# Norm statistics of an MLP's first pass: from the scheduler's places to fixed turns behind the change of pairs

## The chip, the core and the metric

The kernel runs on one core of a Trainium2 chip. The metric is the device time of one execution in microseconds (us). The engines are called by the names of the profile: PE is the matrix engine (TensorE), DVE is VectorE, ACT is ScalarE, POOL is GpSimd, and SP is the engine that issues most of the transfers (DMAs). Each engine works through its own instructions in order and waits where an instruction needs a result of another engine.

## The reference

The input x has 4 sequences of 1024 rows with 128 columns. Four blocks follow each other, each adding its result to x:

```
x = x + attention(layernorm(x))     # 16 heads of 8; each row sees the last 32 rows
                                    # and every 64th row before it; softmax
x = x + mlp(layernorm(x))           # "pass a": 128 (as x and -x) -> 512 -> 512 -> 128, weights +1 or -1
x = x + mamba(x)                    # a state-space block: norm, projection, convolution, a scan
                                    # over time with 16 states, gate, projection, its own residual
x = x + mlp(layernorm(x))           # "pass b" and "pass c": the same MLP again
```

A layernorm needs two numbers of each row, its mean and its variance; the row is then scaled by (variance + 1e-5) to the power -1/2 and shifted. These two numbers are the statistics that this case is about: those of the MLP's first pass, over x as the attention has left it.

## The kernel before

**Tiles.** x stays on the chip. The sequences form two pairs; a tile is 128 partitions, which hold 64 rows of each of the pair's two sequences, by 128 columns, and each pair has 16 such tiles, `xs[0]` and `xs[1]`. Four neighbouring tiles form a chunk (c = 0 to 3 in a pair).

**Attention.** The function `attention` (L201) runs a pipeline written out by hand, the loop at L546 over turns i. In turn i it works on several tiles at once, at different stages: the scores and the softmax of tile i, the strided products of tile i-1, the weights of tile i-2, the values of i-3, the division of i-4 and the residual of i-5, which adds the projected result to x. The tiles 0 to 15 are those of the first pair and 16 to 31 those of the second, so pairs change at turn 16, and tile t of the first pair is final behind the residual in turn t+5. In a pair's tile m the products with every 64th row have m columns of heads: POOL's multiplications (`product`, rows prod; `strided_products`, rows prodv) and DVE's sums over them (rows S<-prod and or<-prodv) grow with m from nothing to 15 x 128 elements, and start again at nothing when the pair changes. prod and prodv share three buffers, so POOL cannot run far ahead of DVE. On DVE a turn is: the predicated copy of the scores S (L395), the reciprocal and product of `divide`, the sums of `strided`, the product eo of `weights_own`, the residual, and `softmax_scores` (L406): the sum S<-prod, the maximum mx, the subtraction S<-S,mx. ACT then makes the exponentials E. Behind that stand the statistics of the attention's own norm for a later chunk (`stats`, L244: a `bn_stats` and a `bn_aggr` for one tile a turn, rows sta and mva; `scales`, L254: four POOL operations for a chunk, rows rsa).

While `attention` is traced, the helper `InOrder` (L49, flag `keep`) asks the scheduler to keep the program's order. The code behind it is traced without that until the scans.

**The MLP.** `mlp` (L685) is a generator that yields a Piece before each group of instructions. Pass a over the first pair is four units, `early(0, c, ...)` for c = 0 to 3 (L784), two in each of two lanes (L1289). Without given statistics it first runs `ln_stats` (L181), which yields four pieces: `bn_stats` and `bn_aggr` on DVE for the chunk's four tiles (two pieces, rows st_fa and mv_fa, L177 and L178), four POOL operations (one piece, rows rs_fa, L187 to L190) and an empty piece. Then come the scaled tiles (fxna), their transposes (ftpa), the first layer (pfa, evicted to h1a), the second (pga, to h2a), the third (pfoa) and the residual (x<-pfoa). The units of the second pair, `early(1, c, ...)`, have their statistics made ahead by `stats_ahead` (L776) and wait for them in `awaited` (L780), a single piece.

As the four units of the first pair stand in no kept order, the scheduler moves their statistics up to where their input is final: tile t's `bn_stats` and `bn_aggr` lie in turn t+5 on DVE, between the operations of `softmax_scores`, and each chunk's four POOL operations lie behind the chunk's last tile, at 72, 105, 139 and 160 us.

**The prologue.** Behind the attention, at L1301, the two lanes and the first units of the mamba block (`mamba_norm`, `mamba_pre_half`, rows mtp, mxn, pc, px, pd, dt, du) are run in turn, a piece of each at a time, until the first mamba unit is prepared. This interleaving counts pieces. It is not by time, and it ends when the scans can start.

**The scans.** `scans` (L1083) goes through 128 units (8 parts of half a sequence x 16 states). For each, POOL makes db, ACT da, DVE two scans hs and a product hc (with pcc from PE), POOL sums pairs of hc, and PE adds these up (pys). Between the units, `pieces` (L1244) places what is left of the MLPs and the other mamba units, by a planner with costs for each engine, in a fixed order. What is still left when the last unit has been placed comes behind it: the tail, with the last mamba output (pmo), and the last MLP units. The transposes of these units are the rows ftpc.

The names that the change and the steps of the prediction touch: `ln_stats`, `early`, `awaited`, `known` (L774), the loop at L546, and the interleaving at L1307. The lines that say how many pieces go in turn:

```python
            wanted = first[-1].may() and "pe" in first[-1].next.us
            for w in first + ([] if wanted else lanes):
                if w.may():
                    w.run()
```

Of the kernel before, what the change touches and what calls it, by code (L numbers as in the profile page):

```python
# [16 lines left out]
F32 = mybir.dt.float32  # L17
# [5 lines left out]
ALU = mybir.AluOpType  # L23
# [3 lines left out]
P = 128  # L27
# [3 lines left out]
NT = T // R  # L31
# [4 lines left out]
EPS = 1e-5  # L36
# [7 lines left out]
def hybrid_kernel(ctx: ExitStack, tc: tile.TileContext, x, Wq, Wk, Wv, Wo, ln_g, ln_b, W_in, conv_w,  # L44
# [17 lines left out]
    ve, te, sc, gp = (InOrder(e) for e in (nc.vector, nc.tensor, nc.scalar, nc.gpsimd))  # L62
    const = ctx.enter_context(tc.tile_pool(name="const", bufs=1))
    xpool = ctx.enter_context(tc.tile_pool(name="xpool", bufs=1))
    small = ctx.enter_context(tc.tile_pool(name="small", bufs=4))
# [15 lines left out]
    xs = []  # L81
    for bp in range(NP):
        t = xpool.tile([P, NT, C], F32, tag=f"x{bp}", name=f"x{bp}")
# [22 lines left out]
    def load_mlp():  # L106
        for t, k in ((k0s, k0), (k1s, k1), (k2s, k2)):
            nc.sync.dma_start(t, k.rearrange("(i p) f -> p i f", p=P))
        for i, s in enumerate((s0, s1, s2, res_scale)):
            nc.sync.dma_start(scal[:, i : i + 1], s.partition_broadcast(P))  # L110
# [35 lines left out]
    minus_half = const.tile([P, 8], F32, name="minus_half")  # L146
# [47 lines left out]
    def ln_apply(dst, src, scale, bias):  # L194
        for i in range(src.shape[1]):
            sc.activation(
                dst[:, i, :], src[:, i, :], AF.Identity, bias=bias[:, i : i + 1], scale=scale[:, i : i + 1]
            )


    def attention(actx):  # L201
# [32 lines left out]
        def weights_in():  # L234
            wt = spare("wt")
            for i in range(4):
                te.transpose(wt[:, i * C : (i + 1) * C], wsrc[:, i], ident)
            sc.copy(wqkv.rearrange("p i c -> p (i c)"), wt[:, : 3 * C])
            sc.copy(woT, wt[:, 3 * C :])
# [4 lines left out]
        def stats(cc, tiles_of=range(4)):  # L244
            bp, c = divmod(cc, NT // 4)
            if cc not in sums:
                sums[cc] = small.tile([P, 4, 2], F32, tag="mva", name=f"mva{cc}", bufs=2)
            mv = sums[cc]
            for i in tiles_of:
                st = small.tile([P, 6], F32, tag="sta", name=f"sta{cc}_{i}", bufs=2)  # L250
                ve.bn_stats(st, xs[bp][:, 4 * c + i, :])
                ve.bn_aggr(mv[:, i, :], st)

        def scales(cc):  # L254
            mv = sums.pop(cc)
            rs = norms[cc] = small.tile([P, 2, 4], F32, tag="rsa", name=f"rsa{cc}", bufs=2)
            gp.tensor_scalar_add(rs[:, 0], mv[:, :, 1], EPS)
            gp.tensor_tensor(rs[:, 0], rs[:, 0], minus_half[:, :4], ALU.pow)
            gp.tensor_scalar_mul(rs[:, 1], mv[:, :, 0], -1.0)
            gp.tensor_mul(rs[:, 1], rs[:, 1], rs[:, 0])  # L260
# [92 lines left out]
        def scores(i):  # L353

            bp, m = tiles[i]
            qT, kx = prep[i // 4][:2]
            q0 = i % 4 * P
            before_tile = prep[(i - 1) // 4][1][:, (i - 1) % 4] if m else None
            ps = psum["s", i] = pw.tile([P, H, 2, W], F32, name=f"ps{i}", tag="ps")
            for g in range(4):  # L360
                rows = slice(g * W, (g + 1) * W)
                for hf in range(2):
                    ch = slice(hf * 64, hf * 64 + 64)
                    heads = slice(hf * HB, (hf + 1) * HB)
                    q = qT[ch, q0 + g * W : q0 + (g + 1) * W]
                    te.matmul(
                        ps[rows, heads, 0, :], q, kx[ch, i % 4, :, g * W : (g + 1) * W], start=True, stop=True
                    )
                    if g % 2:
                        before = kx[ch, i % 4, :, (g - 1) * W : g * W]  # L370
                    elif m:
                        before = before_tile[ch, :, (g + 1) * W : (g + 2) * W]
                    else:
                        continue
                    te.matmul(ps[rows, heads, 1, :], q, before, start=True, stop=True)
            S[i] = ap2.tile([P, H, W + NT - 1], F32, name=f"S{i}", tag="S")

        def keep_scores(i):
            sc.copy(S[i][:, :, :W], psum["s", i][:, :, 0, :])
# [97 lines left out]
        def spread_values(cc, heads):  # L477
            vr = prep[cc][3]
            for a in heads:
                rows = slice(a * W, (a + 1) * W)  # L480
                src = vr[rows].rearrange("k g (j a d) -> k (g j) a d", j=4, d=HD)
                dst = vbs[cc % 2][rows].rearrange("k g j c -> k (g j) c")[:, :, :W]
                dst = dst.rearrange("k j (a d) -> k j a d", d=HD)
                sc.copy(dst[:, :, a], src[:, :, a])
# [53 lines left out]
            ve.tensor_add(xs[bp][:, m, :], xs[bp][:, m, :], psum.pop(("y", i))[:, :C])  # L538


        LEAD = 7

        starts = {(3 if cc == 1 else 4 * cc) - LEAD: cc for cc in range(len(tiles) // 4)}
        preps = []
        last = len(tiles)
        for i in range(-LEAD, last + 5):  # L546
            def at(k, stage):
                if 0 <= i + k < last:
                    stage(i + k)

            if i == -LEAD:
                weights_in()
            if i == 0:
                load_mlp()
            at(-1, strided_products)
            at(1, product)
            at(-2, weights)
            at(0, scores_before)
            at(-4, divide)
            at(-2, strided)  # L560
            at(-2, weights_own)
            at(-2, weights_all)
            at(-2, weights_before)
            at(-5, project_out)
            at(-5, residual)
            if i == 3 - LEAD:
                scores(0)
                keep_scores(0)
            if i >= 0:
                at(1, scores)  # L570
                at(1, keep_scores)
            at(0, softmax_scores)
            at(0, softmax_exp)
            if i in starts:
                preps.append(prep_steps(starts[i]))
            for p in preps:
                next(p, None)
            at(-4, turn_out)
            at(-3, values)
            at(-4, keep_out)  # L580
            for p in preps:
                next(p, None)
            cc, step = divmod(i + LEAD, 4)
            if cc + 2 < last // 4:
                stats(cc + 2, range(step, step + 1))
                if step == 3:
                    scales(cc + 2)
            cc, step = divmod(i + 1, 4)
            if 0 <= cc < last // 4:
                spread_values(cc, range(step, step + 1))  # L590

    with ExitStack() as actx:
        keep.append(True)
        attention(actx)
        keep.clear()
# [89 lines left out]
    def mlp(u, tiles, split, pool, lane, own=None, soon=False, hasty=False, stats=None):  # L685
# [32 lines left out]
        yield Piece(sc=1.6)  # L718
        xn = fx.tile([P, nt, C], F32, name=f"fxn{u}", tag=f"fxn{lane}", bufs=1)
        ln_apply(xn, tiles, stats[:, 0], stats[:, 1])  # L720
        yield fill(0.8)
        tp = bank(f"ftp{u}")[:, :cols]
# [47 lines left out]
        xc = tiles.rearrange("p m c -> p (m c)")  # L770
        ve.scalar_tensor_tensor(xc, po, total, xc, ALU.mult, ALU.add)


    known = {}  # L774

    def stats_ahead(key, needs, tiles_of, soon=False):  # L776
        yield Piece(ready=lambda: all(k in fed for k in needs), same=True)
        known[key] = yield from ln_stats(tiles_of(), "f" + "_".join(map(str, key)), soon)

    def awaited(key):  # L780
        yield Piece(ready=lambda: key in known, same=True)
        return known[key]

    def early(bp, c, *args):  # L784
        stats = (yield from awaited(("a", bp, c))) if bp else None
        tiles = xs[bp][:, 4 * c : 4 * c + 4, :]
        yield from mlp(f"a{bp}_{c}", tiles, True, *args, hasty=bp == 1 and c < HALF, stats=stats)
        fed.add(("a", bp, c))
# [78 lines left out]
    def mamba_norm(bp, c):  # L867
# [21 lines left out]
        yield Piece(sc=1.6)  # L889
        xn = fx.tile([P, 4, C], F32, name=f"mxn{u}", tag="mxn", bufs=1)  # L890
        ln_apply(xn, tiles, rs[:, 1], rs[:, 3])
        if c % HALF == 0:

# [7 lines left out]
        for i in range(4):  # L901
            te.transpose(tp[:, i * P : (i + 1) * P], xn[:, i, :], ident)
        yield Piece(sc=1.6, same=True)
        ln_apply(tiles, tiles, rs[:, 0], rs[:, 2])
        yield evict(sc=0.6)
        t0 = DC - 1 + c % HALF * 4 * R
# [376 lines left out]
    def in_scan_buffers(u):  # L1283
# [5 lines left out]
    lanes = [  # L1289
        Work(stream(  # L1290
            early(0, lane, f1, lane, *[in_scan_buffers] * lane),
            early(0, 2 + lane, f1, lane),
            early(1, lane, f1, lane),
            early(1, 2 + lane, f1, lane),
            *(late(0, 2 * q + lane, f1, lane) for q in range(CT // 2)),
# [95 lines left out]
```

## Time and profile before

| What | us |
| --- | --- |
| median of 4 executions | 908.99 |
| lowest and highest | 908.34 and 911.04 |
| the profiled execution's own time | 911.04 |
| its span, from the first to the last instruction | 909.3 |
| last residual of the attention begins | 247.4 |
| first scan (hs) begins | 323.86 |
| last product of the scans (hc) begins | 867.1 |
| first to last hc | 540.8 |

| Engine | busy us | share of the span |
| --- | --- | --- |
| PE | 749.4 | 82% |
| DVE | 754.0 | 83% |
| POOL | 746.4 | 82% |
| ACT | 595.6 | 65% |

No engine is full over the whole span, so the stages have to be read one by one. In a row of the time view, the first number is the start in us from the span's start, the second the busy time of the row's instructions (xN of them), then come the engine, the line (always L57, the helper that issues everything), the operation, the written and the read tile with their shapes, and in brackets how long the engine had been idle before and which instruction ended that. Matrix products in 32-bit floats count as several instructions in the profile: a `x8` of the program's order is `x16` there for most of them.

### The profile page before, as it was taken

The numbers are of one execution on the slowest core, as the hardware profiler recorded it, in microseconds if no ns is written. First come the engines' busy times: TensorE is split into PE (matmuls) and PEld (weight loads), VectorE is DVE, ScalarE is ACT, GpSimd is POOL, SyncE is SP. The second block draws the span as 40 slices with busy tenths as digits, with TensorE's granted clock in tenths as the row PEclk, the third lists the DMA queues.
The fourth block names the chain that finished last, engine by engine and source line by source line (L and its number), as shares of the span: only waits on it lengthen the run. The fifth ranks groups of instructions, "written<-read, shape, count | busy, mean of one in ns | idle before, by whom it ended". The sixth has DMA issues, their size and how long they took to land.

```text
span 909.3 us, 15374 instructions
## 1 busy us (share of the span) xinstructions
PE 749.4 (82%) x5682; PEld 449.2 (49%) x5682; DVE 754.0 (83%) x1010; ACT 595.6 (65%) x1326; POOL 746.4 (82%) x582
## 2 busy tenths in 40 slices
PE   5797858965688978878889698978989969888888
PEld 2454435643466544334446344545635526555557
DVE  6699898999653279988899999978999998999942
ACT  4776537753254488877877777967779877544523
POOL 6699996999642099999989999988999999988810
PEclk9898869997589999788989999999999999999999
DMA  4633123330010021111111112111122122221100
GB/s 127 127 71 72 27 50 70 74 69 2 20 29 1 1 93 71 70 66 52 70 48 70 61 55 72 67 49 59 59 82 71 47 82 71 81 79 61 36 6 19
DMA packets 47147, 53.11 MB, mean 58 GB/s; under 512 B 4808, under 2 KB 38384, under 8 KB 47072
## 3 DMA queue, kind: packets, MB, share of 16 engines
q1 hardware_dynamic: 45904, 51.59, 19.9%
q8 instruction: 45, 0.74, 0.3%
q0 software_dynamic: 608, 0.27, 0.2%
q10 hardware_dynamic: 560, 0.26, 0.1%
q14 instruction: 30, 0.25, 0.1%
HBM read 45.82 MB, written 4.46 MB: 55 GB/s over the span
## 4 chain that ended last, share of the span: by engine, by line
DVE 32%; PE 22%; POOL 22%; ACT 12%; issue 8%; DMA 2%; SPq 1%; DVEq 0%; POOLq 0%; ACTq 0%
DVE hs L57 14%; POOL db L57 7%; DVE hc L57 5%; PE pga L57 4%; DVE S L57 4%; POOL hc L57 4%; POOL prod L57 3%; PE pys L57 3%; POOL prodv L57 3%; ACT da L57 3%; PE pgc L57 2%; ACT L57 2%; DVE or L57 2%; POOL ep L57 2%; PE pfoa L57 1%
## 5 line engine op out<-in xcount | busy, mean ns | idle before, releaser
L57 POOL TENSOR_TENSOR db<-du,bs 128x1024 f32<-128x1024 f32 x128 | 303.1, 2369 | 0.6 <-DMA bs<-bd 0.6
L57 ACT ACTIVATE da<-dt,a_t 128x512 f32<-128x512 f32 x256 | 175.2, 687 | 112.1 <-DVE hs L57 111.3
L57 POOL TENSOR_TENSOR hc<-hc,hc 128x512 f32<-128x512 f32 x128 | 163.4, 1277 | 28.1 <-DVE hc L57 28.1
L57 DVE TENSOR_TENSOR hc<-hs,pcc 128x1024 f32<-128x1024 f32 x128 | 156.1, 1219 | 20.3 <-PE pcc L57 12.2
L57 DVE TENSOR_TENSOR_SCAN hs<-da,db 128x512 f32<-128x512 f32 x128 | 149.8, 1210 | 18.2 <-ACT da L57 11.1
L57 DVE TENSOR_TENSOR_SCAN hs<-da,carry,db 128x512 f32<-128x512 f32 x128 | 157.0, 1270 | 3.1 <-POOL db L57 1.5
L57 PE MATMUL pys<-hc,ident 128*128 128x512 f32 x256 | 144.9, 651 | 5.3 <-POOL hc L57 5.1
L57 PE MATMUL pcc<-bc,spread 96*128 96x512 bf16 x128 | 50.9, 398 | 38.6 <-DVE hc L57 37.5
L57 PEld LDWEIGHTS pys<-hc,ident 128*128 128x128 f32 x256 | 48.5, 205 | 54.6 <-issue 27.9
L57 PE MATMUL pga<-h1a,w 128*128 128x512 f32 x256 | 73.8, 440 | 0.6 <-ACT h1a L57 0.3
L57 POOL TENSOR_TENSOR prodv<-vS,E 128x128 f32<-128x128 f32 (+14 forms) x30 | 69.5, 2317 | 5.3 <-ACT E L57 5.1
L57 POOL TENSOR_TENSOR prod<-kv,qs 128x128 f32<-128x128 f32 (+14 forms) x30 | 71.2, 2372 | 3.0 <-DVE or L57 2.9
L57 ACT ACT_TABLE_LOAD x48 | 61.6, 1283 | 3.4 <-issue 2.6
L57 PEld LDWEIGHTS pga<-h1a,w 128*128 128x128 f32 x256 | 51.2, 202 | 24.3 <-issue 5.1
L57 PE MATMUL pc<-mxnT,w_conv 128*128 128x512 f32 x128 | 60.0, 594 | 2.8 <-ACT gate L57 2.8
L57 ACT ACTIVATE E<-S 128x512 f32<-128x512 f32 (+15 forms) x62 | 26.5, 473 | 51.7 <-DVE S L57 51.4
L57 PE MATMUL ps<-kx,qT 64*32 64x256 f32 x1008 | 46.3, 437 | 7.5 <-DVE S L57 5.0
L57 PE MATMUL py<-woT,oT 128*128 128x128 f32 x64 | 18.1, 370 | 37.5 <-ACT oT L57 37.2
L57 POOL TENSOR_TENSOR ep<-ep,eo 128x512 f32<-128x512 f32 x32 | 41.1, 1284 | 9.1 <-ACT ep L57 7.8
L57 POOL TENSOR_TENSOR du<-dt,u 128x512 f32<-128x512 f32 x16 | 20.6, 1291 | 28.3 <-ACT dt L57 28.3
L57 ACT COPY ep<-pt 128x512 f32<-128x512 f32 x32 | 18.7, 586 | 38.2 <-DVE eo L57 35.6
L57 DVE TENSOR_REDUCE or<-prodv 128x128 f32<-128x128 f32 (+14 forms) x30 | 36.5, 1218 | 5.1 <-POOL prodv L57 5.1
(234 smaller groups left out, 1596.3 us busy)
## 6 DMA issues: line engine op xcount, KB each, us to landing
bs<-bd SPq DMA_DIRECT2D x64, 512.0 KB
vr<-vd SPq DMA_DIRECT2D x32, 256.0 KB
vd<-kv SPq DMA_DIRECT2D x8, 256.0 KB
x<-in_L_attn_a_x_dram SPq DMA_DIRECT2D x15, 128.0 KB
kx<-kT SPq DMA_DIRECT2D x104, 16.0 KB
out_dram<-x SPq DMA_DIRECT2D x8, 128.0 KB
taps<-in_L_attn_b_conv_w_dram SPq DMA_DIRECT2D x1, 512.0 KB
out_dram<-ox SPq DMA_DIRECT2D x2, 256.0 KB
```

The lines of the kernel that those rows point to most:

```text
L57: ins = getattr(self.engine, name)(*args, **kwargs)
```

## The change

The statistics of the first pair's four chunks are made inside `attention`, in its kept order, and given to the units through `known`. `mlp_stats(t)` makes one tile's `bn_stats` and `bn_aggr` on DVE, `mlp_scales(c)` a chunk's four POOL operations. In the turns 16 to 19 three tiles stand behind the softmax of the turn (tiles 0 to 11), in the turns 20 to 23 one each (tiles 12 to 15). They stand ahead of `turn_out`, `values`, `keep_out` and of the attention's own `stats`. The POOL operations stand at the turn's end, in the turns 17, 18, 19 and 23. The four units in `early` now wait in `awaited`, one piece, where they had four.

```diff
+    known = {}                       # (moved up from behind mlp)
...
+        ready = {}
+
+        def mlp_stats(t):
+            c, i = divmod(t, 4)
+            if i == 0:
+                ready[c] = small.tile([P, 4, 2], F32, name=f"mvm{c}", tag="mvm", bufs=2)
+            st = small.tile([P, 6], F32, tag="sta", name=f"stm{t}", bufs=2)
+            ve.bn_stats(st, xs[0][:, t, :])
+            ve.bn_aggr(ready[c][:, i, :], st)
+
+        def mlp_scales(c):
+            mv = ready.pop(c)
+            rs = known["a", 0, c] = small.tile([P, 2, 4], F32, name=f"rsm{c}", tag=f"rsm{c}", bufs=1)
+            gp.tensor_scalar_add(rs[:, 0], mv[:, :, 1], EPS)
+            gp.tensor_tensor(rs[:, 0], rs[:, 0], minus_half[:, :4], ALU.pow)
+            gp.tensor_scalar_mul(rs[:, 1], mv[:, :, 0], -1.0)
+            gp.tensor_mul(rs[:, 1], rs[:, 1], rs[:, 0])
+
+        stats_at = {NT + k: range(3 * k, 3 * k + 3) for k in range(4)}
+        stats_at.update({NT + 4 + k: range(12 + k, 13 + k) for k in range(4)})
...
             for p in preps:
                 next(p, None)
+            for t in stats_at.get(i, ()):
+                mlp_stats(t)
             at(-4, turn_out)
...
                 if step == 3:
                     scales(cc + 2)
+            for t in stats_at.get(i, ()):
+                if t % 4 == 3:
+                    mlp_scales(t // 4)
...
     def early(bp, c, *args):
-        stats = (yield from awaited(("a", bp, c))) if bp else None
+        stats = yield from awaited(("a", bp, c))
```

More of the change, by code (lines that the diff above doesn't have):

```diff
@@ L771, in mlp @@
         ve.scalar_tensor_tensor(xc, po, total, xc, ALU.mult, ALU.add)
-    known = {}
     def stats_ahead(key, needs, tiles_of, soon=False):
```

## The prediction, on record before the changed kernel was run

> **What bounds the kernel now.** I read the busy share by stage first, then the rows of VectorE (DVE) and GpSimd (POOL) in time order where the statistics stand now, then DVE's waits in the scans, then the chain's end. Busy time by stage (stage, length, busy us and count of PE, PEld, DVE, ACT, POOL, then clock and DMA):
> ```profile
> 130.00:176.00 46.00, 38.16 (x820) 24.30 (x821) 42.63 (x93) 31.79 (x85) 37.65 (x38) 1.00 0.34 67
> 245.70:323.90 78.20, 68.78 (x297) 49.13 (x298) 27.17 (x61) 42.12 (x83) 20.56 (x31) 0.90 0.10 28
> 480.00:568.00 88.00, 74.32 (x298) 42.22 (x297) 83.69 (x79) 67.78 (x148) 86.64 (x72) 0.96 0.17 61
> 868.30:909.30 41.00, 33.66 (x257) 29.62 (x256) 10.69 (x33) 11.98 (x35) 3.74 (x4) 1.00 0.04 14
> ```
> At the change of pairs (130 to 176) DVE is the fullest, POOL has 8 us free; the prologue (246 to 324) and the tail (868 on) are PE's; in the scans DVE and POOL are both near full. DVE in turn 7 of the attention, with a tile's two statistics, and in turn 23, which has the same shapes and none:
> ```profile
> 62.63 1.08 DVE L57 TENSOR_REDUCE S<-prod 128x112 f32<-128x896 f32 x1
> 63.63 0.29 DVE L57 BATCH_NORM_STATS2 st_fa<-x 128x6 f32<-128x128 f32 x1
> 63.83 0.80 DVE L57 TENSOR_REDUCE mx<-S 128x16 f32<-128x624 f32 x1
> 64.53 0.18 DVE L57 BATCH_NORM_AGGREGATE mv_fa<-st_fa 128x2 f32<-128x6 f32 x1
> 64.66 0.80 DVE L57 TENSOR_TENSOR S<-S,mx 128x624 f32<-128x624 f32 x1
> ```
> ```profile
> 173.32 1.08 DVE L57 TENSOR_REDUCE S<-prod 128x112 f32<-128x896 f32 x1
> 174.43 0.81 DVE L57 TENSOR_REDUCE mx<-S 128x16 f32<-128x624 f32 x1
> 175.28 0.80 DVE L57 TENSOR_TENSOR S<-S,mx 128x624 f32<-128x624 f32 x1
> ```
> From the first start to the last it is 2.03 us with the statistics and 1.96 without: they fill the gaps in which mx and the subtraction wait for their inputs, and cost 0.07 us a turn. POOL, where no gap stands from 66.4 to 137, and DVE behind it:
> ```profile
> 105.12 0.54 POOL L57 TENSOR_SCALAR rs_fa<-mv_fa 128x4 f32<-128x4 f32 x2
> 105.62 1.04 POOL L57 TENSOR_TENSOR rs_fa<-rs_fa,minus_half 128x4 f32<-128x4 f32 x1
> 106.74 0.20 POOL L57 TENSOR_TENSOR rs_fa<-rs_fa 128x4 f32<-128x4 f32 x1
> 108.93 3.45 POOL L57 TENSOR_TENSOR prodv<-vS,E 128x1536 f32<-128x1536 f32 x1
> ```
> ```profile
> 112.41 1.75 DVE L57 TENSOR_REDUCE or<-prodv 128x128 f32<-128x1536 f32 x1 [3.08 <-POOL prodv L57]
> ```
> DVE's longest wait in the scans, and PE's rows in the tail:
> ```profile
> 606.15 0.75 DVE L57 SCALAR_TENSOR_TENSOR x<-pfoa,total,x 128x512 f32<-128x512 f32 x1 [4.19 <-PE pfoa L57]
> ```
> ```profile
> 876.72 4.00 PE L57 MATMUL pgc<-h1c,w 128*128 128x256 f32 x32
> 880.56 1.15 PE L57 MATMUL pfc<-fxnTc,w 128*128 128x256 f32 x4
> 882.24 2.05 PE L57 MATMUL pfoc<-w,h2c 128*128 128x128 f32 x16 [0.53 <-ACT h2c L57]
> 884.04 0.72 PE L57 MATMUL pfc<-fxnTc,w 128*128 128x256 f32 x4
> ...
> 891.41 0.66 PE L57 MATMUL ftpc<-ident,fxnc 128*128 128x128 f32 x4 [0.58 <-DVE ox L57]
> ```
> In the tail ftpc, first step of the last MLP, could start near 882, when its input fxnc ends; PE is still on an older unit's matmuls.
>
> **The change part by part.** It moves 32 DVE and 16 POOL instructions and no DMA, and takes three plan pieces out of each of the four first MLP units.
>
> 1. *Attention up to turn 16.* Two groups of four POOL operations (rs_fa at 72.39 and 105.12, 1.82 us each) leave a full engine: 3.64 us. DVE's waits for POOL in turns 14 and 15 (3.08, 1.13, 0.62: 4.83 us) cover that. The 0.07 a turn that DVE saves in turns 5 to 13 (0.6) brings it to its sum at 108.7, just as prodv, 3.64 earlier, ends (108.7). Turn 16 starts 3.7 us earlier. If POOL had not been full from 66.4 on, the gain would be DVE's 0.7 alone; but no gap stands in its rows.
>
> 2. *Turns 16 to 23.* A tile's statistics now stand behind the subtraction, one after another. The nearest row is sta in the same place: 65.38 to 65.80, 0.42 us from start to start. Ends: 0.07, if gaps hide them, and 0.46, the two durations (0.285 and 0.174). I take 0.42, the row of the same two operations in the same place; 16 tiles, 6.7 us. Less 0.3 for the removed pairs in turns 16 to 20, and less the waits that DVE has there anyway (1.67 for ACT's S, 0.76 for PE's pa, 0.39 for S): 2.8 us. DVE is at turn 24 where it was (-3.7 + 6.7 - 0.3 - 2.8 = -0.1). But the last group, rsm3, now stands in turn 23 on POOL in front of prodv23, queued behind it are all products of turns 24 on, and it waits for the last tile's statistics (about 175.9). Its 1.9 us (rsa, the same form, 107.02 to 108.93) end near 177.9, where prodv23 began at 177.02. From there POOL has no gap up to 238.3 and DVE waits for it at the end (0.71, 0.41, 1.66). Attention: **+0.9 us**; ends -2.0 (0.07 a tile) and +1.5 (0.46).
>
> The other three groups, rsm0 to rsm2, cost nothing: 5.7 us in the 8 us that POOL has free from 130 to 176, where its products are short (0.5 to 1.6 us). Without that cover prodv of the same turn would be late by 1.9 us each, as at rsm3. The exponentials on ACT do not wait, since the statistics stand behind the subtraction; what is queued behind them on DVE is the next turn's scores, and behind those ACT's and POOL's work of that turn, which is why the sum is made on DVE.
>
> The Trainium skill (VectorE: DVE Perf Modes, The DRAIN you can't avoid) says that each Vector operation pays its pipeline's drain wherever it stands, with a semaphore or without, so that operations count and not waits. By that the move would be free on DVE; the rows at 62.63 and 173.32 disagree (0.07 in the gaps against 0.42 in a row).
>
> 3. *Prologue.* With three pieces fewer the MLP lanes run ahead of the first mamba unit: in the changed program's PE order 16 pga rows (4.00 us at 317.05) now stand before pd, and pfa and pfoa (1.48 and 3.73) before pc. In return PE fills part of the 3.39 us for which it waited for mxn at 287. Row by row: pc ends 3.2 later; px ends only 0.3 later, since the 3.73 of pfoa no longer lies between them; pd 1.9 later, behind the 16 rows; dt and du 2.0 later; w, and with it bd and bs, which held db until 321.4, come 1.3 earlier, as w waits for no h1a in front of it, and no longer bind; da waits for two more h2a (0.60 each) in front of its table load (1.28). First scan: **+1.5 us**; ends 0 (all in the idle time) and +4.0 (all 16 rows in front of pd). pcc0 behind 16 more rows is ready near 323, before hs needs it.
>
> 4. *Scans.* The same instructions, other places: the pieces come a unit earlier to unit 35, then up to eight units earlier; pfoa and mtp, on whose bank and rows DVE waited in units 65 to 70 (4.19, 1.42, 1.39: 7.0 us), are done by unit 57. I take the 4.2 as gone, not the rest, add 1.3 for DVE work from the tail (two h1c, one fxnTc: 0.5, 0.5, 0.3) and 1 for a denser PE in units 36 to 57: **-2 us**; ends -7 (all of it gone) and +8 (next part). SP: the order of bs, bd and out changes at eight places by one or two; its bs issues wait for POOL's db anyway (316.9 us in all), so nothing; if a bs did come late by one issue it would cost its 4.0 us of landing once.
>
> 5. *Tail.* Behind pmo there no longer stand pgc2_10, pfc2_12 and pfoc2_10 (4.00 + 1.15 + 0.72 + half the PE time of two pfoc, 2.0, and the waits 0.53 and 0.2: 8.6 us). But pfoc2_10 and two pfc now stand in front of pmo, which waits for their bank: pmo ends 2.6 later; and the next h2c is waited for, 1 us. **-5 us**; ends -6 (no such wait) and -3 (two more evictions and their pfc, 2 us, in front of pmo).
>
> Sum: 0.9 + 1.5 - 2 - 5 = -4.6. The profiled execution took 911.04 (span 909.3, 1.7 around it), 2.05 over the median 908.99: 906.4 for it, **904.4 for the median**.
>
> **The rivals.**
> *Slower: PE overfull in units 36 to 57.* By the end of unit 57 the changed order has put 8 us more on PE (16 pga 4.0, pfoa 3.4, mtp 0.6) into a stage (480 to 568) in which PE is idle for 13.7 us, 10.2 of them waits for DVE's and POOL's hc. For it: such idle time is where pcc and pys wait and a fill in front of pcc holds DVE, as at unit 22 (3.59). Against: the fill of 8 fits in 13.7. If half lands in front of a pcc (+4) and the stalls of units 65 to 70 only come earlier (+4.2): 904.4 + 8.2 = 912.6. It decides when first to last hc, 540.8 us now, passes about 545.5.
> *No change:* the stalls come back in other units, the scans grow by 2.5 us with the moved DVE work: 909.
> *The move is free on DVE* (0.42 saved a turn, too): turns 16 to 20 save 1.8 more, rsm3 starts 1.8 earlier, the attention is at -0.9: 902.6. Against it the rows quoted in part 2. That is the result by the skill's rule.
> *The order of the MLP's pieces has no effect,* only the attention's: 909.9, against it the changed order itself; it lies within no change.
>
> **How the numbers follow.** Forecast 0.48, free on DVE 0.10, no change 0.16, slower 0.26. A measurement of this kernel can tell about 0.2% (1.8 us) from no change. The first two are faster by more: 0.58. The likeliest one's own range, 899 to 907, comes from ±4 in the scans. All lower ends together give -15 (894), all upper ones +10.5 (919.5); they are not likely to fall together, and the range, 897 to 912.5, leaves out about 1 in 20 below and 1 in 8 above, the slower case's worse half.
>
> **What would show it.** Waits of DVE for prodv at turn 14 gone; S16 about 3.7 us earlier; four groups of three statistics 0.42 apart; prodv23 0.9 later; last residual near 248.6; first scan near 326.3; first to last hc near 539; no x<-pfoa wait of 4 us at unit 65; ftpc 5 us nearer to the last hc. Wrong if the scans' stage grows by more than 4.5 us, if prodv23 stands earlier than 177, or if ftpc still starts 23 us behind the last hc.

## The result, and the profile after

The changed kernel takes 909.01 us (median of 45 runs) where the kernel before takes 910.62 (median of 71 runs on the same chips): ratio **0.9984, 95% interval 0.9976 to 0.9992**, that is 1.5 us faster (0.7 to 2.2). Forecast were 4.6 us, 904.4 for a median of 908.99; by the ratio it is 907.5. The direction is right and the time lies in the range, but only a third of the gain came, and it lies within the 0.2% that were called no change.

The profiled execution took 911.47 us (span 909.6), 2.5 over its median; that of before was 0.4 over the large median. So the two traces side by side hide the gain, and stages have to be compared one by one, at best over several traces with the same order. (The profiles of two of the experiments, gaps_other_order and gaps_hold_one, are of disturbed executions, with granted clocks of 0.64 and 0.55; of these two only the times are used.) By stage, in us:

| Stage | before | after | difference | forecast |
| --- | --- | --- | --- | --- |
| start to the last residual of the attention | 247.44 | 247.13 | -0.3 | +0.9 |
| from there to the first scan (prologue) | 76.42 | 78.45 | +2.0 | +1.5 |
| first to last hc (scans) | 540.81 | 544.87 | +4.1 | -2 |
| last hc to the end (tail) | 42.19 | 36.71 | -5.5 | -5 |

The 2.44 us between the first scan and the first hc, the same in both, stand in no row.

The attention. DVE's rows in time order around turn 14; where before stood a wait of 3.08 us for prodv there is none, and the subtraction of turn 14 begins at 115.08 (119.42 before). Of these 4.34 us, 0.28 stood already at turn 4 (47.53 and 47.81), where the two kernels do not differ yet, and 0.33 at turn 5 (52.79 and 53.12):

```profile
108.22 0.29 DVE L57 TENSOR_TENSOR o<-pa,rden 128x128 f32<-128x128 f32 x1
108.42 1.74 DVE L57 TENSOR_REDUCE or<-prodv 128x128 f32<-128x1536 f32 x1
...
112.06 2.02 DVE L57 TENSOR_REDUCE S<-prod 128x224 f32<-128x1792 f32 x1 [0.84 <-POOL prod L57]
114.12 0.93 DVE L57 TENSOR_REDUCE mx<-S 128x16 f32<-128x736 f32 x1
115.08 0.92 DVE L57 TENSOR_TENSOR S<-S,mx 128x736 f32<-128x736 f32 x1
```

The statistics of turn 16 on DVE, three tiles behind the subtraction, and the last four POOL operations, rsm3, in front of prodv23 (177.02 before):

```profile
133.64 0.29 DVE L57 BATCH_NORM_STATS2 stm<-x 128x6 f32<-128x128 f32 x1
133.96 0.18 DVE L57 BATCH_NORM_AGGREGATE mvm<-stm 128x2 f32<-128x6 f32 x1
134.06 0.26 DVE L57 BATCH_NORM_STATS2 stm<-x 128x6 f32<-128x128 f32 x1
134.36 0.18 DVE L57 BATCH_NORM_AGGREGATE mvm<-stm 128x2 f32<-128x6 f32 x1
134.45 0.27 DVE L57 BATCH_NORM_STATS2 stm<-x 128x6 f32<-128x128 f32 x1
134.75 0.18 DVE L57 BATCH_NORM_AGGREGATE mvm<-stm 128x2 f32<-128x6 f32 x1
134.85 0.26 DVE L57 BATCH_NORM_STATS2 sta<-x 128x6 f32<-128x128 f32 x1
```

```profile
174.82 0.23 POOL L57 TENSOR_SCALAR rsm<-mvm 128x4 f32<-128x4 f32 x1
175.13 1.04 POOL L57 TENSOR_TENSOR rsm<-rsm,minus_half 128x4 f32<-128x4 f32 x1
176.23 0.25 POOL L57 TENSOR_SCALAR rsm<-mvm 128x4 f32<-128x4 f32 x1
176.56 0.21 POOL L57 TENSOR_TENSOR rsm<-rsm 128x4 f32<-128x4 f32 x1
176.72 2.07 POOL L57 TENSOR_TENSOR prodv<-vS,E 128x896 f32<-128x896 f32 x1
```

Three tiles take 1.21 us (133.64 to 134.85). At turn 16 DVE is 4.40 early. The turns 16 to 23 lose 3.0 of that, rsm3 another 1.1: DVE is 1.42 early at turn 24, POOL's prodv23 only 0.30, and from there POOL has no gap until 239, so the attention ends 0.31 early. That is the earlier start and no more: from the subtraction of turn 5 to the last residual it is 194.3 us in both.

The scans. Busy time by stage, before and after, for the units 57 to 80 and 81 to 104 (stage, length, busy us and count of PE, PEld, DVE, ACT, POOL, then clock and DMA):

```profile
564.19:671.58 107.39, 93.16 (x347) 53.01 (x347) 94.92 (x91) 84.51 (x183) 99.04 (x73) 0.95 0.19 65
671.58:767.99 96.41, 86.22 (x315) 45.84 (x314) 90.64 (x84) 77.02 (x163) 95.46 (x70) 0.98 0.20 66
```

```profile
567.61:669.85 102.24, 87.57 (x271) 43.72 (x272) 91.13 (x83) 82.88 (x170) 99.36 (x71) 0.90 0.20 68
669.85:777.12 107.27, 93.86 (x380) 55.17 (x379) 96.97 (x93) 79.02 (x168) 94.63 (x69) 0.95 0.21 67
```

The changed order wins 5.2 us in the units 57 to 80 and loses 10.9 in the units 81 to 104. The stall of 4.19 us at unit 65 is gone, as forecast, and others stand in the units 100 and 101:

```profile
758.78 1.22 DVE L57 TENSOR_TENSOR hc<-hs,pcc 128x1024 f32<-128x1024 f32 x1 [1.52 <-PE pcc L57]
759.92 2.45 DVE L57 TENSOR_TENSOR_SCAN hs<-da,carry,db 128x512 f32<-128x512 f32 x2
764.39 0.75 DVE L57 SCALAR_TENSOR_TENSOR x<-pfob,total,x 128x512 f32<-128x512 f32 x1 [2.02 <-PE pfob L57]
```

Summed from DVE's rows of each unit (other work: everything but hs and hc; waits: the idle times in brackets):

| Units | length before, after | DVE's other work | DVE's waits |
| --- | --- | --- | --- |
| 1 to 56 | 237.9, 239.6 | 23.5, 24.8 | 16.3, 17.1 |
| 57 to 80 | 107.4, 102.2 | 11.9, 7.3 | 10.8, 9.3 |
| 81 to 104 | 96.4, 107.3 | 7.3, 13.9 | 4.2, 8.7 |
| 105 to 127 | 99.1, 95.8 | 16.3, 14.1 | 1.1, 0 |

The tail on PE. pgc2_10, pfc2_12 and pfoc2_10 no longer stand between pmo (ends 884.31) and ftpc:

```profile
883.87 0.44 PE L57 MATMUL pmo_1own<-x,ident 64*64 64x128 f32 x4
884.24 4.00 PE L57 MATMUL pgc<-h1c,w 128*128 128x256 f32 x32
888.08 1.13 PE L57 MATMUL pfoc<-w,h2c 128*128 128x128 f32 x6
889.76 1.38 PE L57 MATMUL pfoc<-w,h2c 128*128 128x128 f32 x10 [0.55 <-ACT h2c L57]
891.72 0.66 PE L57 MATMUL ftpc<-ident,fxnc 128*128 128x128 f32 x4 [0.58 <-DVE ox L57]
```

ftpc begins 18.83 us behind the last hc (872.89), 24.30 before.

### The profile page after: what moved, and what is told of

It reads as the page before. It is cut to its first block, busy times and chain, and to the rows that moved or that the text cites. A ratio compares the mean times of both kernels' runs of the same rounds, so it can differ in the third digit from the quotient of the medians.

```text
span 909.6 us, 15371 instructions
## 1 busy us (share of the span) xinstructions
PE 755.6 (83%) x5682; PEld 456.0 (50%) x5682; DVE 758.0 (83%) x1010; ACT 595.1 (65%) x1326; POOL 746.6 (82%) x582
## 5 line engine op out<-in xcount | busy, mean ns | idle before, releaser
L57 PE MATMUL pga<-h1a,w 128*128 128x512 f32 x256 | 71.1, 429 | 2.7 <-DVE h1a L57 1.9
L57 PEld LDWEIGHTS pc<-mxnT,w_conv 128*128 128x128 f32 x128 | 24.4, 192 | 32.7 <-issue 26.1
## 6 DMA issues: line engine op xcount, KB each, us to landing
x<-in_L_attn_a_x_dram SPq DMA_DIRECT2D x15, 128.0 KB
out_dram<-x SPq DMA_DIRECT2D x8, 128.0 KB
```

The source lines that it names most:

```text
L57: ins = getattr(self.engine, name)(*args, **kwargs)
```

## The experiments

**The two halves alone.** The change does two things: it moves the statistics, and it takes pieces out of four units. Each can be had alone.

```diff
     def early(bp, c, *args):                 # attention_alone, on the changed kernel
         stats = yield from awaited(("a", bp, c))
+        for _ in range(0 if bp else 3):
+            yield Piece()
```

```diff
+    def in_one(pieces):                      # pieces_alone, on the kernel before:
+        yield Piece()                        # runs ln_stats through in one piece
...
     def early(bp, c, *args):
-        stats = (yield from awaited(("a", bp, c))) if bp else None
+        tiles = xs[bp][:, 4 * c : 4 * c + 4, :]
+        if bp:
+            stats = yield from awaited(("a", bp, c))
+        else:
+            stats = yield from in_one(ln_stats(tiles, f"fa{bp}_{c}", False))
```

> The statistics stand in the attention as in the changed kernel, but each of the four first MLP units gets three empty pieces back, so that PE's, ACT's and SP's order is the one of before, and DVE's and POOL's too but for the statistics. Theory (the parts add): the attention ends 0.3 us earlier, as in the changed kernel's trace (247.13 against 247.44), and behind it nothing changes: first scan near 323.6, first to last hc near 541, last hc to the end 42.2 as before; about -0.3 us, ratio 0.9997 to before, no difference that can be measured. Rival (all that the change gains is in the attention, the pieces' order loses): -1.5 us or more, ratio 0.998 or less.

> The statistics stay where the scheduler finds them, as before, but each of the four first MLP units makes them in one piece, so that PE's and SP's order is the one of the changed kernel. Theory (the parts add): attention ends near 247.4, the first scan is 2.0 us later than before counted from there, last hc to the end is 5.5 us shorter (36.7 against 42.2), the scans take 2 to 4 us more, sum -0.5 to -1.5 us, ratio 0.9984 to 0.9995. Rival (all that the change gains is in the attention): slower than before, ratio 1.0005 or more. Rival (the forecast's own sum for the order, prologue +1.5, scans -2, tail -5): -5.5 us, ratio 0.994.

attention_alone: ratio 1.0009 (0.9992 to 1.0025). pieces_alone: 0.9966 (0.9945 to 0.9986). The first shows no gain: its attention ends at 247.1, first to last hc is 542.3, the tail 42.1. The second has the gain (its interval and the changed kernel's overlap): scans 545.3, tail 36.6. So what the change gains comes from the order of the pieces, not from the statistics, and the rival that had it the other way round is out.

**Where the attention loses again.** scales_late moves rsm3 alone to turn 33, behind POOL's last products; stats_apart does that too and gives each three tiles another order.

```diff
             for t in stats_at.get(i, ()):    # scales_late
-                if t % 4 == 3:
+                if t % 4 == 3 and t < 15:
                     mlp_scales(t // 4)
+            if i == last + 1:
+                mlp_scales(3)
```

```diff
             st = small.tile([P, 6], F32, tag="sta", name=f"stm{t}", bufs=2)   # stats_apart, in mlp_stats
             ve.bn_stats(st, xs[0][:, t, :])
+            yield
             ve.bn_aggr(ready[c][:, i, :], st)
+            yield
...
-            for t in stats_at.get(i, ()):
-                mlp_stats(t)
+            steps = [mlp_stats(t) for t in stats_at.get(i, ())]
+            for k in (0, 1, 0, 2, 1, 2) if len(steps) == 3 else (0, 0)[: 2 * len(steps)]:
+                next(steps[k])
```

> The changed kernel with the four POOL operations of chunk 3 moved from turn 23 to turn 33, behind POOL's last products, all else in its order. Theory (they hold prodv of turn 24 and, as POOL has no gap from there, the end of the attention): prodv23 1.4 us earlier than in the changed kernel (175.3 against 176.72), the last residual near 245.8 (247.13), and the same 1.3 us at the end: ratio 0.997 to before. Rival (DVE's place in turn 23 sets it, not POOL): last residual at 247.1, ratio 0.9984 as the changed kernel. Rival (the attention's end does not carry to the kernel's end): residual at 245.8 but ratio 0.9984.

> As the kernel with the late scales, the statistics behind the change of pairs, three tiles a turn, but no bn_aggr stands right behind its own bn_stats: the order in a turn is stats, stats, aggr, stats, aggr, aggr. Theory (an operation that reads its predecessor's result waits for its end, 0.32 us from start to start, where an unrelated one follows 0.09 us before the end): three tiles take 0.87 us in place of 1.21, four turns save 1.3 us; from the subtraction of turn 14 to that of turn 24 63.2 us (64.57 with the late scales, 64.60 in the changed kernel), last residual 1.3 us earlier, ratio 0.9955. Rival (each operation costs its own time wherever it stands): 64.6 us, ratio 0.997.

scales_late: 0.9970 (0.9952 to 0.9987). POOL's rows in turn 24 there:

```profile
173.88 1.29 POOL L57 TENSOR_TENSOR ep<-ep,eo 128x512 f32<-128x512 f32 x1
175.69 2.07 POOL L57 TENSOR_TENSOR prodv<-vS,E 128x896 f32<-128x896 f32 x1 [0.51 <-ACT E L57]
```

This whole trace stands 0.4 to 0.5 us later than the changed kernel's from its start on (turn 14 at 115.56), so distances are compared: from turn 24's subtraction to the last residual 66.42 us, 67.45 in the changed kernel, 66.34 before. rsm3 costs about 1.0 us at the end of the attention: over all traces that distance is 67.0 to 67.5 with it in turn 23 and 65.9 to 66.4 without. stats_apart: 0.9951 (0.9936 to 0.9965); from turn 14 to turn 24 63.83 us, 64.57 with the late scales. DVE's rows of one group:

```profile
131.31 0.48 DVE L57 BATCH_NORM_STATS2 stm<-x 128x6 f32<-128x128 f32 x2
131.70 0.17 DVE L57 BATCH_NORM_AGGREGATE mvm<-stm 128x2 f32<-128x6 f32 x1
131.90 0.29 DVE L57 BATCH_NORM_STATS2 stm<-x 128x6 f32<-128x128 f32 x1
132.11 0.30 DVE L57 BATCH_NORM_AGGREGATE mvm<-stm 128x2 f32<-128x6 f32 x2
132.33 0.27 DVE L57 BATCH_NORM_STATS2 sta<-x 128x6 f32<-128x128 f32 x1
```

The same six operations take 1.02 us (131.31 to 132.33) in place of 1.21. The order counts, 0.74 us over the four turns, half of what was expected: the third bn_stats still waits for the buffer that the first bn_aggr reads.

**The statistics in the gaps.** gaps puts bn_stats in front of the maximum and bn_aggr behind it, one tile a turn in the turns 5 to 20, in kept order; rsm0 to rsm2 stay in the turns 17 to 19, rsm3 in turn 33. The cut shows where they go in; `mlp_stats` yields between its two operations, its tiles get buffers of their own, and the calls in the turns 16 to 23 are gone.

```diff
+            t = i - 5                        # gaps, in softmax_scores
+            steps = mlp_stats(t) if 0 <= t < NT else iter(())
+            next(steps, None)                # bn_stats
             mx = pw.tile([P, H], F32, name=f"mx{i}", tag="mx")
             ve.tensor_reduce(mx, s[:, :, :n], AX.X, ALU.max)
+            next(steps, None)                # bn_aggr
...
```

> As the kernel with chunk 3's scales in turn 33, but each tile's statistics stand in the gaps of the softmax, in the turns 5 to 20 (bn_stats ahead of the maximum, bn_aggr behind it) as before the change; the scales of chunks 0 to 2 stay in the turns 17 to 19. Theory (a tile's statistics cost 0.07 us there and 0.42 in a row): turn 16 starts 3.6 us earlier than before, nothing of it is spent in the turns 16 to 23, last residual near 243.8 (247.44 before); with the changed kernel's order behind it -4.8 us, ratio 0.9947. Rival (statistics cost the same wherever they stand): last residual near 245.8, as with the late scales alone, ratio 0.997. Rival (the attention's end does not carry): ratio 0.9984.

Ratio **0.9931 (0.9905 to 0.9958)**, the fastest of all: 4.8 us under the changed kernel by the two ratios. DVE's rows of a turn:

```profile
62.41 0.28 DVE L57 BATCH_NORM_STATS2 stm<-x 128x6 f32<-128x128 f32 x1
62.61 0.79 DVE L57 TENSOR_REDUCE mx<-S 128x16 f32<-128x624 f32 x1
63.31 0.17 DVE L57 BATCH_NORM_AGGREGATE mvm<-stm 128x2 f32<-128x6 f32 x1
63.44 0.80 DVE L57 TENSOR_TENSOR S<-S,mx 128x624 f32<-128x624 f32 x1
```

The last residual stands at 243.28 (247.44 before), 4.2 us earlier, but 1.2 of that stood at turn 5 already (51.91 and 53.12). From the subtraction of turn 5, that of turn 16 comes after 80.8 us (84.3 before), that of turn 24 after 125.0 (128.0), the last residual after 191.4 (194.3). The three later kernels with the statistics in the gaps give 190.4 to 190.9 for the last. So 3.0 to 3.9 us of the attention are gone: what POOL's eight operations free (3.64 by the forecast) arrives, and nothing is spent again. With the order's own gain that is 4.5 to 5.4 us, inside the interval of the whole kernel (3.8 to 8.7).

**The order of the pieces.** Only the pieces of the units of chunks 2 and 3 are varied: in the traces one and three of them give the changed order of PE, ACT and DVE in the scans and the tail, four the order of before. On the kernel gaps:

```diff
     def early(bp, c, *args):
-        stats = yield from awaited(("a", bp, c))
+        if bp:
+            stats = yield from awaited(("a", bp, c))
+        else:
+            for _ in range(1 if c < 2 else 4):   # gaps_old_order; 3: gaps_pd_first; 0: gaps_other_order
+                yield Piece()
+            stats = known["a", bp, c]
```

> The statistics in the softmax's gaps and chunk 3's scales late, as in the run before with them (residual at 243.28), but with three empty pieces back in the units of chunks 2 and 3, which gives PE the order of the kernel before. Theory (attention and order add, the order is worth what its stages show: prologue -0.6, scans -3.1, tail +5.5 against the changed kernel's order): last residual near 243.3, first to last hc near 541.6, last hc to the end 42.1, in all 4.2 us less than before, ratio 0.9955, and 1.5 to 3 us more than the same attention with the changed order. Rival (the order is worth nothing): the same time as with the changed order, ratio 0.993.

> The statistics in the gaps, and two empty pieces back in the units of chunks 2 and 3: PE's order in the scans and the tail, and all other engines' but some ACT evictions, is the changed kernel's, but in the prologue pc stands ahead of pfoa, and pd ahead of all 16 pga rows. Theory (in the changed kernel's prologue pd, late by 1.9 us behind pga rows, holds the first scan): the first scan comes 1.4 us earlier after the last residual (bs, which held db until 321.4 before the change, is the next to bind), scans 544.7 and tail 36.7 as in the changed order, ratio 0.9915. Rival (the first scan waits for ACT's evictions of pga and its table load, or for pcc0 behind the same matmuls): no earlier, 0.993, or later.

> The statistics in the gaps, and one piece fewer still in the units of chunks 2 and 3 than in the changed kernel: one more third layer (pfoa) lies in the prologue, the scans have a third order, and in the tail PE has the same rows behind the last scan as before the change (pgc2_10 and pfc2_12 behind pmo). Theory A (the tail is what stands behind pmo, whatever was done ahead): tail 42.1 and ftpc 24.3 behind the last hc, as before, though the prologue has done more. Theory B (work done ahead shortens the tail): tail 36.7 or less. The scans: A leaves them between 540 and 546, as the planner's places fall; by B they are near 541. Prologue 0.5 to 3.4 us longer than the changed kernel's. Ratio 0.992 to 1.001.

gaps_old_order: 0.9956 (0.9940 to 0.9971), as expected, 2.3 us slower than gaps by the ratios, though the intervals overlap; scans 539.7, tail 42.1. gaps_pd_first: 0.9973 (0.9957 to 0.9989), a miss: pd stands ahead of the 16 pga rows, yet dt, at 315.77, is no earlier behind the last residual (71.6 us; 70.1 to 72.3 in the other traces), and the first scan comes 84.81 us behind it, 6 to 9 later than in the others. ACT's rows there:

```profile
315.77 0.69 ACT L57 ACTIVATE dt<-pd,bdt 128x512 f32<-128x512 f32 x1
...
326.26 0.60 ACT L57 ACTIVATE h2a<-pga 128x512 f32<-128x512 f32 x1 [1.26 <-PE pga L57]
326.87 1.28 ACT L57 ACT_TABLE_LOAD   x1
328.17 1.30 ACT L57 ACTIVATE da<-dt,a_t 128x512 f32<-128x512 f32 x2
```

da stands behind every h2a of the prologue in ACT's queue. The first scan is the last h2a plus 2.7 us in all three (321.08 to 323.86 before, 322.89 to 325.58 after, 326.26 to 328.95 here): what sets it is the end of the prologue's pga on PE, not pd. Its tail is that of the changed order (36.6), but its scans take 541.1 us, 2.8 to 4.5 less than the other traces of that order, with the same rows in the same order on DVE and PE; what differs is said at the end of the next part. gaps_other_order: 1.0041 (1.0023 to 1.0058), slower than any expected; where the time lies was not seen, and the two theories of the tail stay untested.

**Why the scans grew.** Two theories on the waits in the units 81 to 104 were tried. One lightens PE: the same two orders without half of pass b's second layer.

```diff
                         yield more(2.05 if split else 1.8)
+                    if u[0] == "b" and i in (1, 2):      # before_light_b and after_light_b
+                        continue
                     w = wt(w1[:, i, (f0 + f) * P : (f0 + f + 1) * P])
```

> The kernel before, with half of the matmuls of pass b's second layer left out (two of four for each output, 64 pgb rows of 128; part of the MLP is not computed), all instructions else in their order. Before: units 81 to 104 take 96.4 to 98.0 us with 4.2 to 5.9 us of DVE's waits in them. Expected of both theories: the waits there fall a little, to 2 to 4 us, the scans take 536 to 541 us; it is the measure for the run beside it.

> The changed kernel with the same matmuls of pass b's second layer left out. In the changed order the units 81 to 104 take 107.3 to 109.2 us, 8.7 to 10.5 us of them DVE's waits (4.2 to 5.9 before), 6.6 us of DVE's other work that lay in other units before. Theory (the waits come from PE, which has 94 to 96 us of work there against 86 to 89, at a granted clock of 0.91 to 0.95 in units 81 to 88 against 1.00): with 17 us of PE's work gone from units 73 to 110 the waits in units 81 to 104 fall to 3 to 5 us, the difference between the two orders there to that of the moved DVE work (6.6 us), and first to last hc is within 1 us of the lightened kernel before. Rival (they come from other engines' work that now falls into the same units: ACT's table loads and dt, POOL's du): the waits stay above 8 us and the scans stay 3 us longer than the lightened kernel before.

before_light_b: 0.9981 (0.9966 to 0.9997), scans 537.9. after_light_b: 0.9984 (0.9968 to 1.0), scans 544.4, waits in the units 81 to 104 10.5 us, not 3 to 5. The stage of these units:

```profile
663.58:772.68 109.10, 91.06 (x349) 52.01 (x348) 97.15 (x93) 79.05 (x168) 94.32 (x69) 0.92 0.21 65
```

PE has 91.1 us of work there where the changed kernel has 93.9, and the stage is no shorter (109.1, 107.3). That does not clear PE's amount of work: PE still has 4.8 us more than before the change (86.2), and its granted clock was lower than in the changed kernel's own trace (0.92, 0.95). In the order of before, at nearly one clock (0.97 in gaps_old_order, 0.96 here), the same matmuls left out take the units 81 to 104 from 98.1 to 96.0 us and the waits in them from 5.8 to 3.9. The other theory takes the MLP's pieces away from the first units of two parts (gaps_hold_two), or of one (gaps_hold_one).

```diff
             while w.may() and not w.next.evict and w.next.banks <= left:
+                if w in works[-2:] and not forced and not w.next.same and now[0] in (80, 81, 82, 83, 84, 96, 97, 98, 99, 100):
+                    break                    # gaps_hold_one: 96 to 100 alone
```

> The statistics in the softmax's gaps and the changed order up to unit 80; the planner gives no new MLP piece to the units 81 to 85 and 97 to 101, the first ones of two parts, where the changed order has 14 groups of MLP matmuls among the old part's last sums, gates and the new part's pd and DVE waits 8.1 us in all (5 of it for pys, pcc and pfob). The pieces come later. Theory (MLP matmuls in front of pys and pcc at a part's start make these waits): DVE's waits in units 81 to 104 fall from 10.4 to 5 us or less, first to last hc 541 or less; the tail grows, by the rows that now stand behind pmo (pgc2_10's last of four, pfc2_12, pfoc2_10), from 36.6 to 39 to 41. Sum within 2 us of the run with the gaps alone, ratio 0.992 to 0.995. Rival (the old and new parts' own chores, ACT's table loads, dt and du, make them whatever MLP does): waits stay at 8 us or more, first to last hc 543 or more, ratio 0.996.

> The same, with MLP pieces held only in the units 97 to 101. Theory: waits in units 97 to 104 fall from 3.5 to 1 us or less, those in units 81 to 96 stay at 6.9; first to last hc near 542.5, tail 38 to 41, ratio 0.993 to 0.996. Rival: waits in 97 to 104 stay at 3 us or more.

gaps_hold_two: 0.9971 (0.9948 to 0.9994). The waits for pys and pfob at the parts' start are gone, but pcc's take their place: waits of 8.9 us in the units 81 to 104 (10.3 in gaps). DVE's products there:

```profile
677.07 1.22 DVE L57 TENSOR_TENSOR hc<-hs,pcc 128x1024 f32<-128x1024 f32 x1 [1.78 <-PE pcc L57]
...
682.94 1.22 DVE L57 TENSOR_TENSOR hc<-hs,pcc 128x1024 f32<-128x1024 f32 x1 [2.40 <-PE pcc L57]
```

In front of these pcc PE had pd, pys<-u, pmo and the sums, the parts' own work, with no MLP among them; from 666.0 to 676.5 its granted clock was 0.51. The scans are 2.1 us shorter than in gaps (541.8) and the tail 6.3 longer (42.9). gaps_hold_one: 1.0026 (1.0010 to 1.0043), a miss; where its time lies was not seen. gaps_hold_two loses more at the end than it wins in the scans; of gaps_hold_one only the whole is known.

A third possibility, PE's granted clock, was given no run, but the traces differ in it. The units 81 to 104:

| Traces | granted clock | length | DVE's other work | DVE's waits |
| --- | --- | --- | --- | --- |
| before | 0.98 | 96.4 | 7.3 | 4.2 |
| attention_alone, gaps_old_order | 0.97 | 98.1 | 7.3 | 6.0, 5.8 |
| gaps_pd_first | 0.97 | 105.5 | 13.9 | 7.0 |
| after | 0.95 | 107.3 | 13.9 | 8.7 |
| pieces_alone, scales_late, gaps, stats_apart | 0.93 | 109.1 to 109.2 | 13.9 | 10.3 to 10.5 |

The first two rows have the order of before, the others the changed one. Within an order, the lower the clock, the longer the waits. At one clock, 0.97, the orders differ by 7.4 us, and 6.6 of that is DVE's other work. The wait of 1.52 us shown above, at 758.78 of the changed kernel, stands behind a stretch (753 to 757) with a clock of 0.57; in gaps_pd_first the clock is 1.00 from 746 to 760, and the same product has no wait:

```profile
758.46 1.22 DVE L57 TENSOR_TENSOR hc<-hs,pcc 128x1024 f32<-128x1024 f32 x1
```

No run changes the clock alone, and why the changed order is granted less of it there is not known.

## Why the prediction was wrong

The parts by the traces with one order are these. The order of before (before, attention_alone, gaps_old_order): scans 540.8, 542.3, 539.7, tail 42.1 to 42.2. The changed order (after, pieces_alone, scales_late, gaps, stats_apart): scans 543.9 to 545.6, tail 36.6 to 36.7; gaps_pd_first, with a longer prologue in front, 541.1 and 36.6. So the order is worth +4.0 in the scans by the five traces (+3.3 with the sixth) and -5.5 in the tail; with nothing in the attention that is -1.5 (-2.2), and -1.5 was measured (-0.7 to -2.2). That the sign came out right is partly luck: the scans were missed by 6 us, and a right tail outweighed them by 1.5.

1. *Attention up to turn 16: right, 0.4 low.* Counted from turn 5, -4.1 in place of -3.7 (the -4.4 of the rows holds the earlier start). The two POOL groups are worth 1.9 each (prodv8 2.37 early, prodv12 4.28). prodv7 is 0.46 early; 0.33 of that is the start, and the rest, which DVE had saved by then, adds to them, where the forecast took it to be covered.
2. *Turns 16 to 23: right in kind, 0.6 too dear.* The statistics stand 0.42 apart (0.39 to 0.46, 6.6 us for 16 tiles), all 2.8 us of waits are used up, the loss is 3.0, not 3.6. rsm3 does hold prodv23, and scales_late prices it at 1.0 us. Counted from turn 5, prodv23 stands where it stood (123.9 us in both), not 0.9 later: attention 0, not +0.9. That prodv23 stands earlier than 177 (176.72), named as a sign of being wrong, is the earlier start. That a tile's statistics cost the same wherever they stand, the rival *the move is free on DVE*, is refuted: six operations take 1.21 us in a row, 1.02 in another order, and about 0.2 in the gaps of three turns (0.07 a turn). The rule of the Trainium skill (VectorE: DVE Perf Modes, The DRAIN you can't avoid), that leaving out semaphores saves nothing and operations count, does not hold for these operations. The same section adds that a next operation that is not held starts earlier; with that the rows agree (0.08 us before the end where nothing of the operation in front is read).
3. *Prologue: the row-by-row sum was a good copy of one trace, and the effect is not shown.* pd 1.8 later, dt 1.9, da 1.8, as forecast. But over the traces the prologue takes 76.4, 77.3, 78.0 and 78.0 us with the order of before (before_light_b the fourth) and 76.3 to 78.5, mean 77.4, with the changed one: the same mean. The granted clock differs among them as well (0.88 to 0.91 and 0.88 to 0.93; the shortest, 76.3, has 0.93, the longest, 78.5, has 0.88). So neither the +2.0 of the first pair nor the +1.5 of the forecast is shown, and an effect of 1 us is not ruled out.
4. *Scans: this step failed.* "I take the 4.2 as gone, not the rest": -2 was forecast, +4.0 came. The stall at unit 65 did go, yet DVE's waits in the units 57 to 80 fall by 1.5 us only (10.8 to 9.3): others, for db and pmo, come in their place. And the forecast took the head start of three pieces to last. It does not: by the end of unit 80 the changed program has 656 matmul instructions of the MLP behind it, counted from the attention's end, where the one before has 696, though it was ahead up to unit 56 (592 against 544). Pass a's last pfoa stands at unit 57 (65 before), but pass b's first scaled tiles, fxnb, at unit 65 (64 before), and the second group of its statistics at 65 (55 before): the head start ran into seven units without MLP work. DVE's other work in the units 57 to 80 falls by 4.6 us; it comes back in the units 81 to 104 (+6.6), and waits of 4.5 us with it in this pair of traces, of 1.0 to 1.2 where the clock was the same. In all, other work +1.2 and waits +2.7 (means of three and five traces) make up 3.9 of the 4.0; in gaps_pd_first the other work is +1.2 too, the waits are -0.6, and the scans are as long as before (+0.2). The mechanism of the rival *no change*, that the stalls come back in other units, fits best, with a price of 2.5 that five of the six traces pass; the tail's gain kept the sum on the fast side. The rival *slower* is out in its place: the units 33 to 56 hold 3.0 us of waits, 3.7 before, and first to last hc is 544.9 (one trace of six passes 545.5, with 545.6).
5. *Tail: right.* -5.5 (forecast -5): ftpc 5.47 nearer to the last hc; pmo ends 1.7 later (2.6), and the next h2c is waited for 0.55 (1).

The waits in the units 81 to 104 are located, not explained: the MLP's matmuls in the first units of a part alone do not make them (gaps_hold_two: 8.9 us without them, at a granted clock of 0.90), PE's amount of work is not cleared (after_light_b), and PE's granted clock goes with them, untested. What belongs to the order for certain is DVE's moved work, 6.6 us in these units in all six traces. Which order of the parts' own work and the MLP's would avoid the waits stays open. What the runs do show is the trade: what leaves the tail, 5.5 us, is paid for in the scans in all but one trace, with 4.0 in the changed order and, the other way round, 2.1 won against 6.3 lost with gaps_hold_two.

The likeliest case's own range in the prediction, 899 to 907 "from ±4 in the scans", is not centred on 904.4; ±4 gives 900.4 to 908.4. The full range does not rest on it.

## What to carry to other kernels

An operation that fits into the time in which its engine waits for its own last result costs next to nothing (0.07 us a pair here), and the same operations in a row cost nearly their whole length (0.42 of 0.46): find the gaps before taking work out of them, and give the engine that has none the relief (here POOL: gaps kept 3.0 to 3.9 us of the 4.1 that the change won by turn 16 and spent again). Where a schedule counts steps rather than time, taking a step out moves everything behind it; price that order as a change of its own, and run the halves apart. Work taken off the end of a kernel whose middle is full on two or three engines can be paid for in the middle, as 4.0 of 5.5 us were here: count it there before the gain at the end is booked. And compare stages of two traces only with the start and the granted clock of each beside them.

## What was not expected of the hardware

On DVE an operation that reads the result of the one in front of it starts 0.03 us behind its end (133.64 + 0.29 to 133.96), one that doesn't starts some 0.08 before it (62.41 + 0.28 to 62.61). That 0.11 us, three times, is 0.33 of the 0.35 us by which a pair is cheaper in the gaps (0.42 and 0.07), and twice it is what stats_apart wins in a group (0.19). And executions differ in their parts: between traces of one order the start up to turn 14 varies by up to 2.8 us (112.8 to 115.6), the prologue by 2.2 (76.3 to 78.5), the scans by 4.5 (541.1 to 545.6), the tail by 0.1; so a single pair of traces tells a 2 us difference only in the stages that don't scatter.
